# Expert tiles: second bias read from the kept table by a register, eight buffers for weight copies, and a fixed order of the steps on two engines

## The chip, the cores and the metric

The kernel runs on one core of a Trainium2 chip. The metric is device time in microseconds, the median of three runs. A core has a matrix engine (TensorE, PE in the profile), an element-wise engine (VectorE, DVE), an engine for activation functions (ScalarE, ACT), a general engine that here issues the indirect transfers and masks (GpSimd, POOL), and SyncE (SP), whose queue here issues all other DMAs. Each engine takes its own queue in order; engines wait for each other by semaphores.

## The reference

The input x is 8 x 512 x 128 in float32. Three blocks follow each other, each with a residual: half a feed-forward layer, attention with 16 heads of 8, and half a feed-forward layer again. The feed-forward layer routes each row to 2 of 8 experts:

```python
xn = (x - mu) * jax.lax.rsqrt(var + EPS) * ln_gamma + ln_beta
abel_out = _gelu(xn @ abel_w + abel_b)
logits = xn @ moe_gate_w + moe_gate_b
topw, topi = jax.lax.top_k(logits, K)
topw = jax.nn.softmax(topw, axis=-1)
...
h = _gelu(jnp.einsum('bsd,edh->ebsh', xn, ew1) + eb1[:, None, None, :])
eo = jnp.einsum('ebsh,ehd->ebsd', h, ew2) + eb2[:, None, None, :]
moe_out = jnp.einsum('ebsd,bse->bsd', eo, w_dense)
for i in range(NROT):
    moe_out = moe_out @ expm(gens[i])
...
mixed = abel_out * (1.0 - gate) + moe_out * gate
```

An expert has weights of 128 x 256 and 256 x 128 and two biases. The three rotations are the same for all rows, so the kernel multiplies them into the second weights and the second bias once.

## The kernel before

**A table of experts.** `rec` (line 130) is kept in SBUF: for each of 8 experts, 645 floats in each of 128 partitions. They are the first weights, the first bias, the second weights times the rotations (from `E_W2`) and the second bias times the rotations (129 floats from `E_B2` to `RECORD`, the same in every partition). The 129th column serves the gate.

**Sorting.** The 8 batches are two groups of 4. For each group `f_sort` (line 364) computes where each of a row's two copies goes, so that rows of one expert lie together in slots of 256 rows. There are 23 slots (`TILES`), and `whose` tells the expert of each slot. `f_send` (line 461) scatters rows to `xd` in DRAM by GpSimd.

**Expert tiles.** `f_experts(n, g, ...)` (line 504) runs the 23 tiles of layer n and group g, so there are four stretches of 23 tiles, 92 in all. A step s of its loop does four things: `fetch(s + 4)` (line 508) loads the expert's number from `whose` into a register of SyncE (L509), copies the record that it names from `rec` into a buffer `r` (L511) and loads the 256 rows `xr` from DRAM (L513); `turn(s)` transposes the rows on TensorE (`px`) and scales them on VectorE (`xs`, L532); `first(s - 1, ...)` multiplies by the first weights (`ph`) and takes the gelu on ScalarE (L546); `second(s - 3)` (line 550) multiplies by the second weights (`po`), adds the bias on VectorE (`y`, L561) and stores to `yd` in DRAM (L564). Records have 5 buffers (`AHEAD + 1`), `xr` 5, `y` 3.

**Gathers and mixes.** When a group's tiles are done, `f_fetch` (line 588) gathers each row's two results from `yd` by GpSimd, 8 gathers a batch (L599), and `f_mix` (line 604) weighs and adds them on VectorE (L613 to L624). In the first layer a batch's buffers `ye` have one copy, in the second two. In the program's text the first group's four mixes stand between the two stretches of tiles of a layer, and in the second layer each mix is followed by the store of the output (L628), by SyncE. In the first layer the second group's mixes are tasks within attention (line 884), which writes the maxima of each unit through SyncE (`qs<-mr`, L940).

**What sets the order.** A scheduler orders each engine's instructions by its own costs. `pin` (line 181, `tc.keep_in_program_order`) keeps instructions in the order of the text among those pinned on the same engine. Pinned before are all matrix products and transposes, GpSimd's gathers, scatters and masks, and one activation; VectorE's and SyncE's work around the expert tiles is not.

Of the kernel before, what the change touches and what calls it, by code (L numbers as in the profile page):

```python
# [8 lines left out]
F32 = mybir.dt.float32  # L9
I32 = mybir.dt.int32  # L10
AF = mybir.ActivationFunctionType
ALU = mybir.AluOpType
# [4 lines left out]
P = 128  # L17
# [4 lines left out]
NE = 8  # L22
# [9 lines left out]
SLOTS, CHUNKS = 256, 2  # L32
TILES = (2 * GROUP * S + NE * (SLOTS - 1)) // SLOTS
AHEAD = 4
# [4 lines left out]
PO = P + 1  # L39
E_B1, E_W2 = NHH * P, NHH * P + NHH  # L40
E_B2 = E_W2 + NHH * PO
RECORD = E_B2 + PO
# [14 lines left out]
def tile_macaron(  # L57
# [19 lines left out]
    nc = tc.nc  # L77
    V, A, G, T = nc.vector, nc.scalar, nc.gpsimd, nc.tensor
# [51 lines left out]
    rec = const.tile([P, NE, RECORD], F32, name="rec", tag="rec")  # L130
# [15 lines left out]
    for i in range(2):  # L146
# [5 lines left out]
        out=mask_q[:, S - P :], in_=mask_q[:, S - P :], pattern=[[-1, P]],  # L152
# [10 lines left out]
        out=less, in_=less, pattern=[[1, P]], compare_op=ALU.is_gt, fill=-1.0,  # L163
# [11 lines left out]
        out=before_e, in_=before_e, pattern=[[1, NE], [-1, NE]], compare_op=ALU.is_gt, fill=0.0,  # L175
# [5 lines left out]
    pin = tc.keep_in_program_order  # L181

    def mm(*args, **kw):
        pin(T.matmul(*args, **kw))  # L184

    def tp(*args):
        pin(T.transpose(*args))  # L187
# [315 lines left out]

    def f_experts(n, g, pools, tasks):
        whose = sorts[n, g][1]
        got, key = {}, f"back{n}_{g}"

        def fetch(t):
            e = nc.sync.value_load(whose[0:1, t : t + 1], min_val=0, max_val=NE - 1)  # L509
            r = pools["sb"].tile([P, RECORD], F32, name=f"r{n}_{g}_{t}", tag="record", bufs=AHEAD + 1)  # L510
            nc.sync.dma_start(out=r, in_=rec[:, bass.ds(e, 1), :].rearrange("p o c -> p (o c)"))  # L511
            xr = pools["sb"].tile([P, CHUNKS, P], F32, name=f"xr{n}_{g}_{t}", tag="xr", bufs=AHEAD + 1)
            d = nc.sync.dma_start(  # L513
                out=xr,
                in_=xd[g][t * SLOTS : (t + 1) * SLOTS, :].rearrange("(c p) d -> p c d", p=P),
            )

            for name in sent[n, g]:
                tc.add_manual_dep(
                    d.ins, name,  # L520
                    mybir.DependencyInfo(mybir.DependencyClass.Sync, mybir.DependencyReason.DATA),
                    reason="sorted rows",
                )
            got[t] = [r, xr]

        def turn(t):
            r, xr = got[t]
            pt = pools["misc"].tile([P, CHUNKS, P], F32, name=f"px{n}_{g}_{t}", tag="misc")
            for c in range(CHUNKS):
                tp(pt[:, c, :], xr[:, c, :], ident)  # L530
            xT = pools["sb"].tile([P, SLOTS], F32, name=f"xs{n}_{g}_{t}", tag="xsT", bufs=3)
            V.tensor_scalar(  # L532
                xT, pt.rearrange("p c q -> p (c q)"),
                cs[:, C_GAMMA : C_GAMMA + 1], cs[:, C_BETA : C_BETA + 1], ALU.mult, ALU.add,
            )
            got[t].append(xT)

        def first(t, c):
            r, xT = got[t][0], got[t][2]
            if c == 0:  # L540
                got[t].append(
                    pools["sb"].tile([P, NHH, SLOTS], F32, name=f"hs{n}_{g}_{t}", tag="hs", bufs=3)
                )
            ph = pools["hid"].tile([P, S], F32, name=f"ph{n}_{g}_{t}_{c}", tag="hid")
            mm(ph[:, :SLOTS], r[:, c * P : (c + 1) * P], xT, start=True, stop=True)
            A.activation(  # L546
                got[t][3][:, c, :], ph[:, :SLOTS], AF.Gelu, bias=r[:, E_B1 + c : E_B1 + c + 1]
            )

        def second(t):  # L550
            r, hs = got[t][0], got[t][3]
            po = pools["out"].tile([P, CHUNKS, PO], F32, name=f"po{n}_{g}_{t}", tag="out")
            for c in range(CHUNKS):
                for k in range(NHH):
                    mm(
                        po[:, c, :], hs[:, k, c * P : (c + 1) * P],
                        r[:, E_W2 + k * PO : E_W2 + (k + 1) * PO],
                        start=(k == 0), stop=(k == NHH - 1),
                    )
            y = pools["sb"].tile([P, CHUNKS, PO], F32, name=f"y{n}_{g}_{t}", tag="y", bufs=3)  # L560
            V.tensor_tensor(  # L561
                y, po, r[:, E_B2:RECORD].unsqueeze(1).to_broadcast([P, CHUNKS, PO]), ALU.add
            )
            nc.sync.dma_start(  # L564
                out=yd[g][t * SLOTS : (t + 1) * SLOTS, :].rearrange("(c p) d -> p c d", p=P),
                in_=y,
            )
            del got[t]

        for t in range(AHEAD):  # L570
            fetch(t)
        for s in range(TILES + 3):
            if s + AHEAD < TILES:
                fetch(s + AHEAD)
            if s < TILES:
                turn(s)
            if 0 <= s - 1 < TILES:
                first(s - 1, 0)
                first(s - 1, 1)
            if 0 <= s - 3 < TILES:  # L580
                second(s - 3)
            for f, *args in tasks.pop(s, ()):
                f(*args)
        assert not tasks

    back = {}
# [43 lines left out]
    def f_first(between):  # L630
# [52 lines left out]
        with ExitStack() as ph:  # L683
            pools = f_pools(0, ph)
            f_experts(0, 0, pools, {})
            for b in groups[0]:
                for t in range(TT):
                    f_fetch(0, b, t, work, 1)
                f_mix(0, b, False)
            f_experts(0, 1, pools, between(pools["misc"]))  # L690
# [9 lines left out]
    def f_second():  # L700

        with ExitStack() as ph:
            pools = f_pools(1, ph)
            n, b = 1, NB - 1
            sides = {b: f_beside(n, b, pools["hid"], pools["misc"], pools["sb"]) for b in range(NB)}

            def side(b):
                next(sides[b], None)

            tasks = {  # L710
                0: [(f_norm, n, b)],
                1: [(f_turn, n, b, pools["misc"])],
                2: [(f_logits, n, b, pools["misc"])],
                3: [(f_sort, n, 1, pools["misc"])],
                4: [(f_send, n, i, t) for i in range(GROUP, NB) for t in range(TT)],
                5: [(f_half, n, b)],
            }
            for i in range(NB):
                tasks.setdefault(5 + 2 * i, []).append((side, i))
                tasks.setdefault(6 + 2 * i, []).append((side, i))  # L720
            f_stats(n, (b,))
            f_experts(n, 0, pools, tasks)
            for b in range(GROUP):
                for t in range(TT):
                    f_fetch(n, b, t, pools["sb"], 2)
                f_mix(n, b, True)
            f_experts(n, 1, pools, {})
            for b in range(GROUP, NB):
                for t in range(TT):
                    f_fetch(n, b, t, pools["sb"], 2)  # L730
                f_mix(n, b, True)
# [449 lines left out]
```

## Time and profile before

| | |
|---|---|
| median of 3 runs | 1014.27 us (1010.85 to 1017.79) |
| profiled execution | 1012.17 us |
| its span | 1010.1 us |
| TensorE busy | 800.7 us (79%) |
| VectorE busy | 546.6 us (54%) |
| ScalarE busy | 446.9 us (44%) |
| GpSimd busy | 348.7 us (35%) |
| first expert stretch | 124.7 to 189.2 us |
| second, with the first group's mixes | 189 to 288 us |
| attention | 288 to 796 us |
| third expert stretch | 796 to 880 us |
| fourth, with the first group's mixes | 880 to 958 us |
| last gathers and mixes | 958 to 1010 us |

The profile is of one execution. A line of a timeline gives the start in us, the duration in us, the engine, the source line, the operation, and what it writes and reads; in brackets stands the idle time of the engine before it and what ended it. A "q" after an engine's name marks its sequencer: waits, register work and DMA issues. A line of waits gives the waiter, whom it waited for, the total in us, how often, and the longest. The stretches in the table are cut at the first record copy and the end of the last `y` of each.

### The profile page before, as it was taken

Reading aid. Unit: us, or ns where it says so; the run is one execution under the profiler, and the core shown is the slowest. Engines: PE = TensorE matmul, PEld = TensorE weight load, DVE = VectorE, ACT = ScalarE, POOL = GpSimd, SP = SyncE. Lnnn points to the kernel's source line nnn. Section 1 sums busy time; section 2 is a strip of 40 time slices with the busy share of each in tenths; the row PEclk is TensorE's granted clock in tenths of the full one; section 3 lists DMA queues with packets and bytes.
Section 4 is the critical chain, followed back from the end, with each engine's and each line's share of the span. In section 5 each row is a group of like instructions: output and inputs, shape, how many; then the busy total and the mean of one; then the engine's idle time right before and its main releaser. Section 6 shows DMA issues by size and latency. Waiting matters only on the chain.

```text
span 1010.1 us, 17346 instructions
## 1 busy us (share of the span) xinstructions
PE 800.7 (79%) x5546; PEld 554.1 (55%) x5546; DVE 546.6 (54%) x2049; ACT 446.9 (44%) x928; POOL 348.7 (35%) x421
## 2 busy tenths in 40 slices
PE   4569888767668689999999967999999779956800
PEld 4469777656545345555555533455655578845800
DVE  5855533254338565676767672676773253445323
ACT  2434233235203355767676732666766434412300
POOL 4277700245034521121212138332111047074075
PEclk9579989978766777999999975999999789978955
DMA  9973166756621300101010101201000346766622
GB/s 259 299 188 75 56 224 221 217 158 178 159 71 25 69 14 11 36 4 43 4 44 3 44 17 49 56 10 42 4 3 2 107 148 217 248 178 179 218 58 68
DMA packets 104010, 101.22 MB, mean 100 GB/s; under 512 B 11424, under 2 KB 80936, under 8 KB 103640
## 3 DMA queue, kind: packets, MB, share of 16 engines
q1 hardware_dynamic: 95728, 83.26, 28.5%
q0 software_dynamic: 8192, 16.86, 6.0%
q8 instruction: 44, 0.72, 0.3%
q14 instruction: 46, 0.38, 0.1%
HBM read 34.37 MB, written 32.89 MB: 67 GB/s over the span
## 4 chain that ended last, share of the span: by engine, by line
PE 65%; DMA 8%; issue 7%; POOL 7%; DVE 7%; SPq 3%; ACT 2%; POOLq 0%; DVEq 0%; ACTq 0%
PE sa L184 18%; PE sb L184 9%; PE py L184 8%; POOL ye L599 6%; PE ph L184 6%; PE po L184 6%; DMA ye<-yd,to 4%; DMA xr<-xd 3%; PE rp L184 3%; PE pl L184 2%; PE pyt L187 2%; PE px L187 2%; PE pp L184 2%; SPq L509 1%; PE ab L184 1%
## 5 line engine op out<-in xcount | busy, mean ns | idle before, releaser
L925 DVE CUSTOM_DVE_ANT_0 junk<-sa,mask_q 128x128 f32<-128x128 f32 (+3 forms) x512 | 251.1, 490 | 146.1 <-PE sb L184 96.4
L184 PE MATMUL sa<-ks,qs 32*128 32x128 f32 (+3 forms) x1024 | 289.9, 514 | 15.4 <-DVE mx L925 15.2
L184 PE MATMUL sb<-qs,ks 32*128 32x256 f32 (+3 forms) x1024 | 284.8, 502 | 5.5 <-DMA qs<-mr 5.5
L964 ACT ACTIVATE pr<-sb 128x384 f32<-128x384 f32 (+1 forms) x384 | 188.6, 524 | 153.9 <-PE sb L184 142.7
L599 POOL DMA_INDIRECT ye<-yd,to x128 | 123.1, 961 | 239.5 <-DMA r<-rec 68.9
L184 PEld LDWEIGHTS sa<-ks,qs 32*128 32x128 f32 x1024 | 126.6, 203 | 117.8 <-DVE mx L925 88.4
L969 POOL TENSOR_SCALAR_AFFINE_SELECT pr<-pr 128x512 f32<-128x512 f32 x128 | 80.0, 637 | 302.5 <-ACT pr L964 302.4
L468 POOL DMA_INDIRECT xd<-xh,to x128 | 125.3, 979 | 110.3 <-issue 34.6
L546 ACT ACTIVATE hs<-ph,r 128x256 f32<-128x256 f32 x184 | 82.7, 474 | 151.9 <-PE ph L184 143.4
L184 PEld LDWEIGHTS sb<-qs,ks 32*128 32x128 f32 x1024 | 136.1, 199 | 18.3 <-issue 8.1
L184 PE MATMUL ph<-xs,r 128*128 128x256 f32 x368 | 113.5, 438 | 38.2 <-issue 24.4
L184 PEld LDWEIGHTS po<-r,hs 128*128 128x128 f32 x736 | 105.2, 208 | 6.0
L184 PE MATMUL po<-r,hs 128*128 128x129 f32 x736 | 104.5, 290 | 0.0
L184 PEld LDWEIGHTS ph<-xs,r 128*128 128x128 f32 x368 | 74.1, 224 | 48.4 <-issue 40.1
L184 PE MATMUL py<-pr,va 128*32 128x512 f32 (+3 forms) x1024 | 94.8, 469 | 2.8 <-POOL pr L969 2.8
L561 DVE TENSOR_TENSOR y<-po,r 128x258 f32<-128x258 f32 x92 | 39.0, 424 | 80.3 <-PE po L184 65.9
L532 DVE TENSOR_SCALAR xs<-px,cs 128x256 f32<-128x256 f32 x92 | 49.6, 541 | 53.9 <-PE px L187 51.5
L613 DVE TENSOR_TENSOR ye<-ye,wts 128x516 f32<-128x516 f32 x32 | 22.0, 696 | 91.2 <-DMA ye<-yd,to 91.2
L187 PE MATMUL px<-ident,xr 128*128 128x128 f32 x184 | 40.7, 308 | 38.0 <-DMA xr<-xd 32.3
L620 ACT ACTIVATE gt<-gt,half_gcb 128x4 f32<-128x4 f32 x16 | 4.7, 296 | 114.9 <-DVE gt L619 114.9
L184 PEld LDWEIGHTS py<-pr,va 128*32 128x32 f32 x1024 | 24.4, 112 | 53.9 <-issue 23.0
L187 PEld LDWEIGHTS px<-ident,xr 128*128 128x128 f32 x184 | 24.1, 156 | 50.2 <-issue 31.8
(185 smaller groups left out, 850.2 us busy)
## 6 DMA issues: line engine op xcount, KB each, us to landing
r<-rec SPq DMA_DIRECT2D x92, 322.5 KB
yd<-y SPq DMA_DIRECT2D x92, 129.0 KB
xr<-xd SPq DMA_DIRECT2D x92, 128.0 KB
xd<-blank SPq DMA_DIRECT2D x2, 2944.0 KB
qkd<-qk SPq DMA_DIRECT2D x16, 256.0 KB
x<-in_x_dram SPq DMA_DIRECT2D x8, 256.0 KB
qs<-in_alibi_q_dram SPq DMA_DIRECT2D x2, 1024.0 KB
ks<-in_alibi_k_dram SPq DMA_DIRECT2D x2, 1024.0 KB
```

Of the source, the lines that this page charges most:

```text
L184: pin(T.matmul(*args, **kw))
L187: pin(T.transpose(*args))
L468: d = G.indirect_dma_start(out=xd[g], out_offset=bass.IndirectOffsetOnAxis(to[:, k, j : j + 1], 0), in_=xhs_f[n, b][:, t, :], in_offset=None,)
L509: e = nc.sync.value_load(whose[0:1, t : t + 1], min_val=0, max_val=NE - 1)
L532: V.tensor_scalar(xT, pt.rearrange("p c q -> p (c q)"), cs[:, C_GAMMA : C_GAMMA + 1], cs[:, C_BETA : C_BETA + 1], ALU.mult, ALU.add,)
L546: A.activation(got[t][3][:, c, :], ph[:, :SLOTS], AF.Gelu, bias=r[:, E_B1 + c : E_B1 + c + 1])
L561: V.tensor_tensor(y, po, r[:, E_B2:RECORD].unsqueeze(1).to_broadcast([P, CHUNKS, PO]), ALU.add)
L599: pin(G.indirect_dma_start(out=back[b][k][:, t, :], out_offset=None, in_=yd[g], in_offset=bass.IndirectOffsetOnAxis(to[:, k, j : j + 1], 0),))
L613: V.tensor_tensor(ys[k], ys[k], wts[:, k, js].unsqueeze(2).to_broadcast([P, TT, PO]), ALU.mult)
L925: V.tensor_tensor_reduce(junk[:, :n], sa[:, at : at + n], mask_q[:, S - n :], 1.0, -3.0e38, ALU.add, ALU.max, mxs[u][:, j, i : i + 1],)
L964: A.activation(pr[:, j, :], sb[:, :width], AF.Exp)
L969: pin(G.affine_select(out=pr[:, :, at : at + P], in_=pr[:, :, at : at + P], pattern=[[0, GH], [1, P]], compare_op=ALU.is_ge, fill=0.0, bas ...
```

## The change

The second bias is no longer part of a tile's copy of the record: the copy ends at `E_B2` (516 floats a partition in place of 645). For the addition of the bias VectorE loads the expert's number from `whose` into a register of its own, and reads 129 floats of `rec` at that place. The record buffers become 8 (`AHEAD + 4`). Both register loads leave out the check of bounds at run time. The loads, the record copy, the load of the rows, `xs`, `y` and the store to `yd` are pinned, so that SyncE and VectorE keep them in the order of the program's text. The mixes and the stores of the output are not pinned. `key`, which is no longer read, goes.

```diff
     def f_experts(n, g, pools, tasks):
         whose = sorts[n, g][1]
-        got, key = {}, f"back{n}_{g}"
+        got = {}
+
+        def expert(t, engine):
+
+            loads, (e,) = nc.values_load_multi_w_load_instructions(
+                whose[0:1, t : t + 1], engines=[engine], min_val=0, max_val=NE - 1,
+                skip_runtime_bounds_check_because="a count of experts, at most NE - 1 by a minimum",
+            )
+            for i in loads:
+                pin(i)
+            return rec[:, bass.ds(e, 1), :].rearrange("p o c -> p (o c)")
 
         def fetch(t):
-            e = nc.sync.value_load(whose[0:1, t : t + 1], min_val=0, max_val=NE - 1)
-            r = pools["sb"].tile([P, RECORD], F32, name=f"r{n}_{g}_{t}", tag="record", bufs=AHEAD + 1)
-            nc.sync.dma_start(out=r, in_=rec[:, bass.ds(e, 1), :].rearrange("p o c -> p (o c)"))
+            r = pools["sb"].tile([P, E_B2], F32, name=f"r{n}_{g}_{t}", tag="record", bufs=AHEAD + 4)
+            pin(nc.sync.dma_start(out=r, in_=expert(t, mybir.EngineType.SP)[:, 0:E_B2]))
...
                 in_=xd[g][t * SLOTS : (t + 1) * SLOTS, :].rearrange("(c p) d -> p c d", p=P),
             )
+            pin(d)
...
-            V.tensor_scalar(
+            pin(V.tensor_scalar(
                 xT, pt.rearrange("p c q -> p (c q)"),
                 cs[:, C_GAMMA : C_GAMMA + 1], cs[:, C_BETA : C_BETA + 1], ALU.mult, ALU.add,
-            )
+            ))
...
-            V.tensor_tensor(
-                y, po, r[:, E_B2:RECORD].unsqueeze(1).to_broadcast([P, CHUNKS, PO]), ALU.add
-            )
-            nc.sync.dma_start(
+            b2 = expert(t, mybir.EngineType.DVE)[:, E_B2:RECORD]
+            pin(V.tensor_tensor(y, po, b2.unsqueeze(1).to_broadcast([P, CHUNKS, PO]), ALU.add))
+            pin(nc.sync.dma_start(
                 out=yd[g][t * SLOTS : (t + 1) * SLOTS, :].rearrange("(c p) d -> p c d", p=P),
                 in_=y,
-            )
+            ))
             del got[t]
```

## The prediction

> **What bounds the kernel now.** I read the page's slices first, then the timeline of each of the four stretches of expert tiles, then the waits and the chain on SyncE's queue. The slices tell that TensorE is nearly full where attention runs and holed around it.
>
> ```profile
> span 1010.1 us, 17346 instructions
> PE   4569888767668689999999967999999779956800
> ```
>
> A slice is 25.25 us. Attention's are nines; the holes that this change touches are slices 7 to 11 (177 to 303 us) and 35 to 37 (884 to 960 us). There the second 23 tiles of an expert layer run beside the gathers and mixes of the first. The timeline of 200 to 210 us shows what holds the tiles:
>
> ```profile
> 202.35 0.94 POOL L599 DMA_INDIRECT ye<-yd,to  x1 [0.31 <-issue]
> ...
> 203.74 0.69 DVE L613 TENSOR_TENSOR ye<-ye,wts 128x516 f32<-128x516 f32 x1 [6.46 <-DMA ye<-yd,to]
> 204.93 0.69 DVE L613 TENSOR_TENSOR ye<-ye,wts 128x516 f32<-128x516 f32 x1 [0.49 <-DMA ye<-yd,to]
> 205.54 0.42 DVE L561 TENSOR_TENSOR y<-po,r 128x258 f32<-128x258 f32 x1
> ...
> 206.48 0.54 DVE L532 TENSOR_SCALAR xs<-px,cs 128x256 f32<-128x256 f32 x1
> ...
> 207.12 2.05 PE L184 MATMUL ph<-xs,r 128*128 128x256 f32 x4 [5.18 <-issue]
> ```
>
> VectorE takes its queue in order. A mix (L613) waits 6.46 us for a gather, the tile's `y` and `xs` stand behind it, and TensorE idles 5.18 us and comes back at half clock (2.05 us; 1.03 elsewhere). Four tiles or so slip through between two mixes: **before, gathers and tiles share the time.**
>
> Where no mix interferes, two paces compete. TensorE's, from its timeline in the last stretch, is 1.98 us a tile:
>
> ```profile
> 932.80 0.38 PE L187 MATMUL px<-ident,xr 128*128 128x128 f32 x2
> ...
> 934.78 0.38 PE L187 MATMUL px<-ident,xr 128*128 128x128 f32 x2
> ```
>
> SyncE's shows on the chain of waits where the first tiles start:
>
> ```profile
> 127.09 0.54 SPq L511
> ...
> 127.67 0.59 SPq L513
> ...
> 128.31 0.63 SPq L509
> ```
>
> Record copy 0.54, rows of x 0.59, register load 0.63: issue alone takes 2.2 us a tile here. Last, SyncE's own waits:
>
> ```profile
> SPq L511 <- DVE y L561: 63.8, 35, 7.1
> ...
> SPq L509 <- DVE whose L451: 15.1, 1, 15.1
> ```
>
> The first is the record copy waiting for a free buffer, the second the load of the second layer's table in the middle of attention.
>
> **The change, part by part.** The sum is made on the profiled execution, 1012.2 us with a span of 1010.1; the median of the runs, 1014.3, is 0.2% above it.
>
> *Eight record buffers, shorter copies.* The 63.8 us of waits go, since a record is fetched 4 steps ahead and released 3 steps after its own. What is late next is SyncE itself. A copy shrinks from 322.5 to 258 KB; the DMA share of the stretches is only 0.60 to 0.67, so I count nothing for it.
>
> *Order on SyncE.* In the changed program's built order each step is load, address, record copy, rows, `yd`. Before, a load mostly came right after a record copy and took 0.27. The bounds operations (0.15 and 0.02, with gaps 0.05 each) go. The new step, by rows of the trace: load 0.62, address 0.05, copy 0.49, rows 0.59, `yd` 0.45, two event waits of 0.03, and 0.04 after each of the seven: 2.54. I take **2.55 us**. Here two rules of the Trainium skill speak against the rows, one each way. "DMA: Bandwidth & Descriptors", section "Issuing engines are not separate DMA queues", says that the sequencer's time to start a DMA is usually small beside the DMA; by it SyncE costs nothing and tiles run at 1.98. Its section "Latency and other measured facts" gives a register load a floor of about 600 ns; the trace has 0.27 for most, so that no floor holds, but 0.58 to 0.63 after two other issues. With 0.27 the step is 2.2. In the changed order the load always follows copy, rows and `yd`, so I stay with 0.62. A fetch without `yd` (the first eight of a stretch) is 1.97.
>
> *Second bias by a register on VectorE.* 92 loads and 92 address operations. The trace has none on VectorE; the nearest row is SyncE's load, 0.26 to 0.90. An added instruction can't gain. VectorE works some 1.0 us in a 1.98 us step, and `y` waits for `po` anyway, so the four products of `po` hide it; only the last three tiles of a stretch, 0.9 us apart, let it show. I take 0; uncovered it is 1 us a stretch.
>
> *Order on VectorE and across stretches.* This is the large term. In the built order all four mixes of the first group stand ahead of the second group's first `xs`; and in the second layer SyncE issues the four output stores, each waiting for its mix, ahead of the second group's first fetch. Queued behind: every tile of the group, TensorE and ScalarE with it.
>
> *First stretch.* First copy issued at 124.66 as before; 8 x 1.97 + 15 x 2.55 = 54.0; the last rows land 1.9 after that issue ends; the last tile's path (0.4 + 0.86 + 0.9 + 0.87 + 2.69 + 0.45) 6.2; handovers 0.4: last `y` ends at 187.2. Before 189.15: **-2**.
>
> *Second stretch.* Gathers start 4.0 later (3.7 to 4.4 in the three other places), 191.2. Per batch the eighth gather starts after 8.75, lands after 2.8, multiply, add and subtract take 1.95, restart 0.4: 13.9 (14.4 to 15.7 before, with tiles between). Four: 3 x 13.9 + 8.75 + 2.8 + 3.3 for the mix's end = 56.5, so the first `xs` is at 247.7. At half clock the first `y` comes 8.3 later, 256.0. SyncE then needs 15 x 2.55 = 38.3, plus 6 for the ten issues of attention's first queries and keys and their landing, then 3.2 landing (up to 5.0 was seen there) and 6.2: 309.7. Before 288.0: **+21.7**, the first stretch included.
>
> *Attention.* The loads that sat in it go. The chain:
>
> ```profile
> 605.62 0.26 SPq L509
> ...
> 606.24 0.64 SPq L940
> ...
> 609.40 1.19 PE sb L184
> ```
>
> The maxima were ready at 599.6 and were sent only at 606.24: up to 6.6 us. But GpSimd's queue is full of scatters from 596.9 on and reaches the next mask only here:
>
> ```profile
> 618.76 0.64 POOL L969 TENSOR_SCALAR_AFFINE_SELECT pr<-pr 128x512 f32<-128x512 f32 x1
> ```
>
> TensorE waits for GpSimd at 626.3, and GpSimd's order is unchanged. I take **0**; if that cover is thinner than it looks, -6.6.
>
> *Third stretch.* TensorE and its side products set 3.26 us a step, more than 2.55. The start loses the loads taken in advance (1.97 a fetch, 1.29 before): **+1**.
>
> *Fourth stretch.* The 32 gathers run 883.8 to 923.6 as before. The last mix ends 45.7 after 883.8 (39.8 + 2.6 + 3.3); store, load and address 0.9; first copy at +46.6; then 62.6 as from 124.66 to 187.2: +109.2. Before 957.75, +73.9: **+35.3**. The closing gathers and mixes, 52.4, stay.
>
> Sum 21.7 + 0 + 1 + 35.3 = 58: **1070 us**.
>
> **The rivals.**
>
> *TensorE's pace.* The hold stays, but SyncE keeps up. First stretch: tile 6 at 141.0, 16 x 1.98 and 6.2: 178.8. Second: 239.3 + 23 x 1.98 + 4.1 of attention's products + 2 half clock + 6.2 = 297, +9. Fourth: 54.1 for 62.6: +26.8. With the third's 1, 1049. For it: the median load of 0.27, and fetches that run ahead while the mixes hold. Against: the rows above.
>
> *Slower still.* A SyncE step of 2.8 (a load of 0.9 was seen once) costs 15 x 0.25 in each of three stretches, VectorE's loads 1 us each: 1084.
>
> *Faster.* The mechanism is that the deeper prefetch carries the second group past the mixes. At SyncE's pace the second stretch would end near 246 and the fourth near 939: -42 and -19, 953. What decides is how many mixes stand ahead of the group: each costs about 14 us in the second stretch and 10 in the fourth, some 29 with the fill; none gives -60, four give +58, and two break even. The built order has four on VectorE, so this needs an order that the chip cannot choose.
>
> **How the numbers follow.** My forecast 0.57, TensorE's pace 0.22, slower still 0.18, faster 0.03. The range takes 1049 less 3 at the low end and 1084 at the high. A measurement of this kernel tells about 1% from no change. Faster by over 1% 0.02, within 1% 0.01, slower 0.97.
>
> **What the changed profile would show.** Right: VectorE's eight long waits for `ye<-yd`, with no `xs` between the mixes; TensorE idle some 55 us from about 192 and some 48 from about 885; `px` 2.5 us apart elsewhere; SyncE's wait for `y` at the record copy gone; no load around 600 us, with TensorE still late on GpSimd after 610. Wrong: `px` 2.0 us apart (then 1049), tiles running between two mixes (then the hold is misread), or attention shorter by more than 3 us.

## The result, and the profile after

The change makes the kernel slower: **1061.63 us**, median of 4 runs (1057.19 to 1065.32), against 1012.56 of the kernel before (4 runs, 1006.23 to 1017.79). The ratio is 1.0486, with an interval of 1.0405 to 1.0566. The profiled execution after took 1065.32 us, with a span of 1063.5; that of before took 1012.17. So the profiles differ by 53.2 us, where the medians differ by 49.1: two of the four runs after took some 7 us less than the other two, of which one is the profiled one.

The page of the kernel after: its span and TensorE's slices of 26.6 us.

```profile
span 1063.5 us, 17340 instructions
PE   4579889106977689999999768999997799009900
```

Where the page of before had fives to eights around 200 and 900 us there are now two holes, a 1 and 0 (slices 7 and 8, counted from 0, 186 to 239 us) and a 0 and 0 (slices 34 and 35, 904 to 957); the last two zeros are the closing gathers, as before. The first six of seven stages of that span, from the kernel after, and then the second and the fourth stretch of the kernel before; the columns after the window and its length are the busy times of PE, PEld (TensorE's weight loads), DVE, ACT and POOL, each with its number of instructions, then the granted TensorE clock (its share of full speed), the DMA share and GB/s:

```profile
0.00:132.13 132.13, 96.58 (x582) 87.54 (x582) 78.44 (x313) 44.18 (x84) 73.51 (x93) 0.77 0.58 167
132.13:188.64 56.51, 49.51 (x322) 44.84 (x322) 20.66 (x46) 20.90 (x46) 0.00 (x0) 0.94 0.67 211
188.64:310.49 121.85, 55.98 (x347) 49.95 (x350) 43.45 (x127) 34.15 (x68) 31.73 (x33) 0.72 0.46 126
310.49:819.69 509.20, 463.85 (x3524) 256.21 (x3518) 317.50 (x1326) 290.73 (x602) 149.89 (x199) 0.89 0.10 25
819.69:904.31 84.62, 72.69 (x452) 63.79 (x452) 37.66 (x113) 35.76 (x75) 30.96 (x32) 0.90 0.52 166
904.31:1011.13 106.82, 49.98 (x322) 45.09 (x322) 36.86 (x87) 22.09 (x50) 30.77 (x32) 0.73 0.48 144
```

```profile
189.15:288.02 98.87, 66.16 (x345) 57.78 (x348) 40.74 (x127) 32.33 (x67) 31.70 (x33) 0.81 0.60 164
...
879.80:957.75 77.95, 54.49 (x318) 49.20 (x318) 35.05 (x87) 21.93 (x50) 31.31 (x32) 0.87 0.67 199
```

Beside the prediction, in us (a stage's length; the stretches end with their last `y`):

| stage | before | after | change | predicted |
|---|---|---|---|---|
| opening, to the first record copy | 124.7 | 132.1 | +7.5 | 0 |
| first stretch | 64.5 | 56.5 | -8.0 | -2 |
| second stretch | 98.9 | 121.9 | +23.0 | +23.7 |
| attention | 507.6 | 509.2 | +1.6 | 0 |
| third stretch | 84.1 | 84.6 | +0.5 | +1 |
| fourth stretch | 78.0 | 106.8 | +28.9 | +35.3 |
| closing gathers and mixes | 52.3 | 52.3 | 0 | 0 |
| sum | 1010.1 | 1063.5 | +53.4 | +58 |

The two holds are where they were expected. The timeline of the kernel after at the end of the first:

```profile
244.38 2.04 DVE L622 TENSOR_TENSOR ye<-ye,wts 128x516 f32<-128x516 f32 x2 [8.14 <-DMA ye<-yd,to]
...
248.07 1.14 DVE L633 SCALAR_TENSOR_TENSOR x<-xT,gt,x 128x128 f32<-128x128 f32 x4
249.12 0.99 DVE L542 TENSOR_SCALAR xs<-px,cs 128x256 f32<-128x256 f32 x2
...
249.71 2.08 PE L184 MATMUL ph<-xs,r 128*128 128x256 f32 x4 [53.72 <-DVE xs L542]
```

The fourth mix ends, the group's first two `xs` follow at once, and TensorE starts after 53.72 us of idle time, at half clock (granted 0.50 from 249 to 253 us). The waits of TensorE from 904 to 960 us show the other hold, and whom it waits for is not the same:

```profile
PE px L187 <- DMA xr<-xd: 54.6, 2, 53.5
```

Here no rows have been fetched: SyncE stands at the output stores. In SyncE's own waits of the kernel after there is none for `y` at the record copy (63.8 us before), and the one of the output stores for the mixes has grown from 50.9 us to:

```profile
SPq L637 <- DVE x L633: 93.9, 8, 18.0
```

Between the holds tiles run faster than forecast. The chain of the kernel after in the fourth stretch, where SyncE sets it (start, us, what):

```profile
968.50 0.23 SPq L522
...
968.82 0.46 SPq L573
...
969.32 0.28 SPq L510
...
969.80 0.49 SPq L520
...
970.34 4.16 DMA xr<-xd
```

The register load (L510) behind the store (L573) takes 0.28, where 0.62 was counted. Record copies are issued 2.19 us apart (median in the first and in the fourth stretch), not 2.55. TensorE runs off at its own 1.98 us a tile, overtakes SyncE, and then stands for one landing of rows, as here: its transposes `px` start 1.99 us apart in the first stretch and 2.05 in the fourth by the median, 2.12 and 2.16 by the mean.

### The profile page after: what moved, and what is told of

Read it like the earlier page. It is cut to its first block, busy times and chain, and to the rows that moved or that the text cites. A ratio compares the mean times of both kernels' runs of the same rounds, so it can differ in the third digit from the quotient of the medians.

```text
span 1063.5 us, 17340 instructions
## 1 busy us (share of the span) xinstructions
PE 788.6 (74%) x5546; PEld 547.4 (51%) x5546; DVE 550.9 (52%) x2049; ACT 449.0 (42%) x929; POOL 347.6 (33%) x421
## 4 chain that ended last, share of the span: by engine, by line
PE 65%; POOL 10%; DMA 9%; issue 6%; DVE 6%; SPq 1%; ACT 1%; POOLq 0%; DVEq 0%; ACTq 0%
PE sa L184 16%; PE sb L184 8%; POOL ye L608 8%; PE py L184 8%; PE ph L184 7%; PE po L184 7%; DMA ye<-yd,to 4%; PE rp L184 3%; DMA xr<-xd 3%; PE px L187 2%; PE pl L184 2%; POOL xd L468 2%; PE pyt L187 2%; PE pp L184 1%; PE ab L184 1%
## 5 line engine op out<-in xcount | busy, mean ns | idle before, releaser
L184 PE MATMUL ph<-xs,r 128*128 128x256 f32 x368 | 104.7, 411 | 53.7 <-DVE xs L542 53.7
L187 PE MATMUL px<-ident,xr 128*128 128x128 f32 x184 | 40.6, 306 | 83.1 <-DMA xr<-xd 80.7
L184 PEld LDWEIGHTS po<-r,hs 128*128 128x128 f32 x736 | 98.0, 196 | 4.6
L184 PEld LDWEIGHTS ph<-xs,r 128*128 128x128 f32 x368 | 68.9, 209 | 60.5 <-DVE xs L542 54.1
L572 DVE TENSOR_TENSOR y<-po,rec 128x258 f32<-128x258 f32 x92 | 39.3, 427 | 114.9 <-PE po L184 74.5
L184 PE MATMUL po<-r,hs 128*128 128x129 f32 x736 | 98.4, 279 | 0.0
## 6 DMA issues: line engine op xcount, KB each, us to landing
qkd<-qk SPq DMA_DIRECT2D x16, 256.0 KB
x<-in_x_dram SPq DMA_DIRECT2D x8, 256.0 KB
```

The source lines that it names most:

```text
L572: pin(V.tensor_tensor(y, po, b2.unsqueeze(1).to_broadcast([P, CHUNKS, PO]), ALU.add))
```

## The experiments

Eleven kernels were run, each beside runs of the kernel before. Four questions: what holds the tiles, what sets SyncE's step, what the other parts of the change are worth, and whether the order can be had without the hold. The first is seen best in the order that VectorE's queue was built with. A dot is a tile's `xs`, an M a mix (where a mix is in pieces, its first):

```
                          second stretch                 fourth stretch
before                    ....M....M....M....M.......    ......M.M..M..M............
after                     MMMM.......................    MMMM.......................
no order (e1)             .....M....M....M....M......    ......M.M..M..M............
order on SyncE only (e2)  ..M.....M....M....M........    MMMM.......................
mixes placed (e3)         .......M.......M....M.....M    ........M.....M.....M.....M
in pieces (e7)            ......M.......M.......M...M    .......M.....M.....M.....M.
```

**No order at all (e1).** All of the change but the pins.

```diff
-            pin(V.tensor_scalar(
+            (V.tensor_scalar(
...
-            for i in loads:
-                pin(i)
```

(So for `xs`, `y`, the loads, the copy, the rows and the store.)

> The change with nothing pinned on VectorE and SyncE; the short copies, the eight buffers and the register on VectorE stay. In the built order the four mixes stand after 5, 9, 13 and 17 of the second group's tiles in the first layer, and after 6, 7, 9 and 11 in the second, nearly as before the change. Theory (the whole loss is the order, the rest of the change costs nothing): about the time of the kernel before, 1005 to 1020 us, second stretch some 99 us from the last y before it to its own last y, fourth some 78. Rival (the register load on VectorE or the shorter, more frequent copies cost): some 10 us more a stretch of tiles, 1030 us or more. Rival (eight buffers free the tiles): faster than before by over 1%, under 1000 us.

Measured: 996.37 us, ratio to before 0.985 (0.971 to 0.999). The two stretches in the kernel without the order:

```profile
187.13:268.56 81.43, 58.69 (x345) 52.09 (x348) 40.71 (x126) 31.82 (x67) 31.71 (x33) 0.87 0.64 179
...
853.82:932.35 78.53, 54.06 (x318) 49.07 (x318) 35.27 (x86) 21.91 (x50) 31.13 (x32) 0.85 0.60 170
```

The whole loss is gone with the order, as the theory has it, and more: the second stretch is 17.4 us shorter than before the change, so that the total comes out as the last rival said. The four runs spread, 986 and 990 us at a mean granted clock of 0.87, 1003 and 1009 at 0.86 and 0.84. What is left of the change is no cost but a gain, of 1.5% over all four runs and some 2.3% in the first two.

**Order on SyncE only (e2).** `xs`, `y` and VectorE's loads are not pinned.

```diff
             for i in loads:
-                pin(i)
+                if engine == mybir.EngineType.SP:
+                    pin(i)
```

> The change with the order kept on SyncE alone; xs, y and the register loads of VectorE are not pinned. In the built order the first layer's mixes stand after 2, 7, 11 and 15 of the second group's tiles, the second layer's four still ahead of its tiles, with the four output stores ahead of the second group's first fetch on SyncE. Theory (two holds with two causes: in the second stretch it is VectorE's order, in the fourth SyncE's stores alone would do it): second stretch back near before's 99 us, fourth still about 107, so 1035 to 1045 us. Rival (VectorE's order makes both): both back, 1010 to 1020. Rival (SyncE's order makes both): both stay, 1060.

Measured: 1027.61 us, ratio 1.016 (1.007 to 1.024). The two stretches:

```profile
185.48:278.70 93.22, 63.98 (x347) 56.12 (x350) 40.94 (x126) 32.09 (x67) 31.70 (x33) 0.82 0.63 165
...
865.51:973.21 107.70, 49.70 (x322) 44.91 (x322) 37.84 (x87) 22.09 (x50) 30.68 (x32) 0.75 0.47 143
```

Second stretch 93.2, fourth 107.7: as the theory said for both, while the total is 7 us below its range, much of it in the first stretch, 58.0 us here and 64.5 before. So the change has **two holds with two causes**. In the first layer VectorE's order makes it. In the second SyncE's order is enough: four output stores, each behind its mix, stand ahead of the next group's fetches, and with no rows there is nothing that VectorE could do first. A kernel with VectorE's order alone was not run, so whether that order is enough for a hold, in either layer, stays open.

**Copies with five buffers (e5).** The kernel of e1 with the old number of buffers.

```diff
-tag="record", bufs=AHEAD + 4)
+tag="record", bufs=AHEAD + 1)
```

> The kernel of the run without order (nothing pinned on VectorE and SyncE), with five buffers for the copies of records in place of eight; short copies and the register on VectorE stay. The mixes stand after 4, 9, 13 and 17 of the second group's tiles in the first layer. Theory (of the second stretch's gain of 17.4 us against the kernel before, 98.9 to 81.4, all is the eight buffers'): SyncE waits for y at the record copy again, second stretch 95 to 99 us, total 1005 to 1020. Rival (the gain is of the shorter copy or of the order that the scheduler now takes): second stretch stays at 81 to 85, total as with eight buffers, 990 to 1000.

Measured: 1006.15 us, ratio 0.990 (0.983 to 0.997), in the range of the first theory. But it doesn't settle the shares. By the ratios 1% of e1's 1.5% is there with five buffers too, and so belongs to the shorter copy or the scheduler's new order. But four of e5's five runs lie at 1003 to 1006 us, and the two shortest of e1 at 986 and 990; by these most of the gain is the buffers'. By the second stretch, 94.3 us here and 81.4 in e1, nearly three quarters of that stretch's gain is the buffers'; but this profile is of the longest of e5's runs (1022.69 us), with a clock of 0.78 in that stretch where e1 had 0.87. Both parts gain something; how much each, stays open.

**Rows ahead of the register load (e4).** To see what SyncE's load costs behind what.

```diff
         def fetch(t):
-            r = pools["sb"].tile([P, E_B2], ..., bufs=AHEAD + 4)
-            pin(nc.sync.dma_start(out=r, in_=expert(t, ...)[:, 0:E_B2]))
             xr = ...
             pin(d)
...
+            r = pools["sb"].tile([P, E_B2], ..., bufs=AHEAD + 4)
+            pin(nc.sync.dma_start(out=r, in_=expert(t, ...)[:, 0:E_B2]))
             got[t] = [r, xr]
```

> The change with one thing moved: each fetch issues the load of the rows ahead of the register load and the record copy, so that SyncE's order is store, rows, register load, copy in place of store, register load, copy, rows. Theory (a register load takes 0.55 to 0.6 us right behind the issue of the rows and 0.27 behind a store to yd or a copy): median load 0.56, the tiles of the last stretch 2.45 us apart for 2.18, that stretch 4 us longer. Rival (the load takes 0.27 whenever SyncE is in its steady pace, whatever stands ahead): median load 0.27, tiles 2.18 apart, no change.

Measured: 1073.21 us in one run; fourth stretch 111.5 us for 106.8, first 61.6 for 56.5, copies 2.50 us apart. The register loads of this kernel, and below those of the change (minimum, median, maximum in ns):

```profile
L510 SPq TENSOR_LOAD <-whose x92: 263/557/867, 131.9 to 1009.5; - x92
```

```profile
L510 SPq TENSOR_LOAD <-whose x92: 262/278/780, 87.8 to 1001.3; - x92
L510 DVEq TENSOR_LOAD <-whose x92: 296/310/609, 141.9 to 1009.8; - x92
```

The theory holds, with the step at its size: with the same short copies the load takes twice as long right behind the rows as behind a store. In its step, 2.50 for 2.55, this kernel is the one that the prediction described.

**The full record with the order (e6), and with the register too (e9).** e6 reads the bias from the tile's copy again, with no load on VectorE; e9 has the long copy and the load.

```diff
-            r = pools["sb"].tile([P, E_B2], ..., bufs=AHEAD + 4)
+            r = pools["sb"].tile([P, RECORD], ..., bufs=AHEAD + 4)
-            pin(nc.sync.dma_start(out=r, in_=expert(t, ...)[:, 0:E_B2]))
+            pin(nc.sync.dma_start(out=r, in_=expert(t, ...)))
...
-            b2 = expert(t, mybir.EngineType.DVE)[:, E_B2:RECORD]
+            b2 = r[:, E_B2:RECORD]
```

(The last two lines in e6 alone.)

> The change with the second bias read from the tile's own copy again: the copy is 645 floats a partition, VectorE has no register load; eight buffers and the order on both engines stay. Theory (the register load on VectorE lies beside its own work, and the shorter copy saves nothing that is waited for): the time of the change, 1055 to 1066 us, tiles 2.18 us apart, the same holds. Rival (a load and an address operation cost VectorE 0.4 us a tile that shows, up to 1 us a stretch in the drain and more where VectorE is busy): 4 to 15 us less than the change.

Measured: 1077.57 us, ratio 1.059 (1.048 to 1.070): 16 us **more** than the change by the medians, 11 by the ratios, which neither theory had. Copies stood 2.46 us apart, and the load behind a store took 0.52 us. That gave the next expectation.

> The change with the record copies of 645 floats a partition; VectorE's register load, eight buffers and the order stay, so that against the run with the full record only the register load is put back. Theory (it is the longer copy that makes SyncE's register load behind a store take 0.52 us in place of 0.27, and so its step 2.46 in place of 2.19): 1070 to 1085 us, load behind a store 0.5, copies 2.46 us apart. Rival (the register load on VectorE in place of the copied bias was what saved time, or those runs had a lower clock): 1055 to 1066, load 0.27, copies 2.19 apart.

Measured: 1077.86 us, ratio 1.064 (1.055 to 1.074). The loads of e9:

```profile
L510 SPq TENSOR_LOAD <-whose x92: 264/532/858, 85.2 to 1005.8; - x92
L510 DVEq TENSOR_LOAD <-whose x92: 299/322/886, 136.9 to 1015.1; - x92
```

With and without VectorE's register load the medians are within 0.3 us (far inside the intervals), and no stretch of tiles is longer in e9 than in e6, so that load costs nothing that shows. The copy's length is worth some 12 to 16 us of the pinned kernel, 12 by the four stretches of e9's profile and 16 by the medians: with 645 floats SyncE's load behind a store takes 0.51 us and the step 2.45, with 516 floats 0.27 and 2.19. Why a longer copy, with the rows and the store issued after it, lengthens a register load isn't shown by any run.

**Mixes placed between the tiles (e3).** All of the change stays; the first group's gathers and mixes become tasks of the second group's steps, pinned, and each output store stands two steps behind its mix.

```diff
+MIX_0 = (6, 13, 20, 25)
+MIX_1 = (7, 12, 17, 22)
...
-            for b in groups[0]:
-                for t in range(TT):
-                    f_fetch(0, b, t, work, 1)
-                f_mix(0, b, False)
-            f_experts(0, 1, pools, between(pools["misc"]))
+            tasks = between(pools["misc"])
+            gather(0, 0, work, 1)
+            for b in groups[0]:
+                tasks.setdefault(MIX_0[b], []).append((f_mix, 0, b, False))
+                if b + 1 < GROUP:
+                    tasks[MIX_0[b]].append((gather, 0, b + 1, work, 1))
+            f_experts(0, 1, pools, tasks)
```

> The change with one thing moved in the text: the first group's mixes (pinned on VectorE) and their gathers are put between the second group's tiles, after 7, 14, 18 and 23 tiles in the first layer and after 8, 13, 18 and 23 in the second; each output store stands two steps behind its mix. Theory (the hold is the loss, and the pinned steps themselves run at some 2.2 us a tile): the second stretch takes 23 x 2.2 and 7 of fill and drain, 58 us for 122, the fourth 59 for 107; a mix takes some 4 us of VectorE of which half shows, 8 us a stretch: 960 to 975 us. Rival (gathers and tiles share the DMA queues or GpSimd so that tiles starve anyway): no better than before, 1005 to 1020. Rival (the pinned order of SyncE is itself the cost): over 1040.

Measured: 982.32 us, ratio 0.972 (0.964 to 0.980). So the pinned order isn't the cost; where the mixes stand in it is. But the two stretches take 79.3 and 76.2 us, not the 66 and 67 that the theory gives with its 8 us of mixes. The timeline of e3 shows what a mix does:

```profile
870.89 1.29 DVE L631 TENSOR_TENSOR ye<-ye,wts 128x516 f32<-128x516 f32 x2
...
874.27 1.14 DVE L642 SCALAR_TENSOR_TENSOR x<-xT,gt,x 128x128 f32<-128x128 f32 x4
875.33 0.54 DVE L544 TENSOR_SCALAR xs<-px,cs 128x256 f32<-128x256 f32 x1
...
875.97 1.33 PE L186 MATMUL ph<-xs,r 128*128 128x256 f32 x4 [2.92 <-issue]
```

It waits for no gather; it just keeps VectorE for 4.4 us, an `xs` stands behind it, and TensorE stops and comes back slower. I had let half of it hide; the fourth stretch exceeds the 59 us without mixes by 17, as much as four whole mixes.

**Mixes in pieces (e7).** `f_mix` becomes four pieces behind the `y` of four steps.

```diff
+            yield
         pin(V.tensor_add(m, m, ys[1]))
...
+                mix = mix_pieces(n, b)
+                for k in range(4):
+                    tasks.setdefault(MIX_1[b] + k, []).append((next, mix))
```

> The kernel with the mixes between the tiles, each mix cut into four pieces that stand behind the y of four successive steps (two products; sum and gate; gate and difference; four updates of x), the first piece after 6, 13, 20 and 23 tiles in the first layer and after 7, 12, 17 and 22 in the second. Theory (in one piece a mix keeps VectorE 4.4 us, xs stands behind it, and four of them are the 17.6 us by which the fourth stretch, 76.2 us, exceeds 23 steps of 2.18 and the fill and drain; in pieces of at most 1.3 us they fit into what VectorE has free of a step): fourth stretch 60 to 64 us, second 64 to 70, total 945 to 960. Rival (gathers that land 8 us after their issue among the tiles' own transfers, or the transfers themselves, set that stretch): no gain over the mixes in one piece, 975 to 985.

Measured: 982.44 us, ratio 0.968 (0.958 to 0.977). The fourth stretch is 65.7 us for e3's 76.2, a little above the theory's 60 to 64. The second, with 83.1, missed it, and so did the total. The timeline of e7 shows why:

```profile
268.15 0.69 DVE L631 TENSOR_TENSOR ye<-ye,wts 128x516 f32<-128x516 f32 x1 [6.44 <-DMA ye<-yd,to]
269.45 0.70 DVE L631 TENSOR_TENSOR ye<-ye,wts 128x516 f32<-128x516 f32 x1 [0.60 <-DMA ye<-yd,to]
270.06 0.42 DVE L574 TENSOR_TENSOR y<-po,rec 128x258 f32<-128x258 f32 x1
```

The fourth batch's two products stand ahead of the last three `y` and wait for their gathers: the change's own fault, in small.

**The old copies with the right order (e8).** e7 with the record of 645 floats, five buffers and no register.

```diff
-            r = pools["sb"].tile([P, E_B2], ..., bufs=AHEAD + 4)
+            r = pools["sb"].tile([P, RECORD], ..., bufs=AHEAD + 1)
```

> The kernel with the mixes in pieces, with the record copies as before the change: 645 floats, five buffers, no register on VectorE; only the order is left of the change. Theory (a record lives from 4 steps ahead of its tile to 3 behind; with five buffers its copy can only go out two steps ahead, and two steps of 2.2 us are just what issue and landing take): SyncE waits for y at the record copy, tiles 2.4 to 2.8 us apart, 8 to 15 us more in each of the three stretches that run at SyncE's pace, 970 to 1000. Rival (with a right order five buffers do as well, the buffers add nothing): within 5 us of the mixes in pieces with eight buffers.

Measured: 1122.74 us, ratio 1.102 (1.092 to 1.112), far beyond both. Copies stand 4.5 us apart in the first stretch. SyncE's waits of e8 for `y` at the record copy, which the change had taken away, and its timeline there:

```profile
SPq L522 <- DVE y L574: 164.6, 65, 7.9
```

```profile
168.60 0.43 DVE L574 TENSOR_TENSOR y<-po,r 128x258 f32<-128x258 f32 x1 [3.69 <-DMA yd<-y]
169.09 0.49 SPq L522 DMA_DIRECT2D r<-rec  x1
169.63 0.58 SPq L524 DMA_DIRECT2D xr<-xd  x1
170.27 0.50 SPq L575 DMA_DIRECT2D yd<-y  x1
...
173.06 0.43 DVE L574 TENSOR_TENSOR y<-po,r 128x258 f32<-128x258 f32 x1 [3.59 <-DMA yd<-y]
```

It is a circle of one tile. The copy waits for a record buffer, which `y` frees; rows and then the store to `yd` are issued behind the copy; the next `y` waits until that store has landed and given one of the three `y` buffers back. The scheduler's order before the change issued the store of tile t - 7 ahead of the copy for tile t, not behind it, and had no such circle. Three things differ from e7; the copy's length was worth 12 to 16 us in e9 and VectorE's load nothing, so most of the 140 us is left to the buffers. With five buffers and no order (e5) the kernel took 1006 us, so a fixed order and the eight buffers belong together: neither can be judged alone.

**Last obstacles (e10), and the stores by another engine (e11).** e10 is e7 with the fourth mix of the first layer behind its stretch, and attention's first transfers behind SyncE's last fetch; e11 adds one word.

```diff
-            15: [(spread, 0, 0, psum)],
-            16: [(spread, 0, 1, psum)],
+            20: [(spread, 0, 0, psum)],
+            21: [(spread, 0, 1, psum)],
...
+            f_mix(0, GROUP - 1, False)
```

```diff
-            pin(nc.sync.dma_start(
+            pin(nc.scalar.dma_start(
                 out=yd[g]...
```

> The kernel with the mixes in pieces, and two things moved in the first layer's second stretch: the fourth batch's mix stands behind the last tile, and the products, transfers and values for attention's first batch are put from steps 15, 16 and 18 to 20, 21 and 22, behind SyncE's last fetch (the first batches' first pieces stand at steps 5, 13 and 21). Theory (that stretch, 83.1 us for 65.7 in the fourth, loses 8 us to SyncE waiting for attention's transfers among its fetches and 11 to the two last y standing behind a product that waits for the fourth batch's gathers): second stretch 64 to 69 us, of which up to 5 come back at the start of attention; total 955 to 968. Rival (the gathers' pace sets it, or attention starts later by as much): no gain, 975 to 985.

> The kernel of the run before in this list with one thing moved: the stores to yd are issued by ScalarE in place of SyncE. Theory (without the stores SyncE's step is 1.97 us, below TensorE's 1.98, though its register load then stands behind the rows and takes 0.56): tiles of the first stretch 2.0 us apart for 2.15, first stretch 3 us shorter, the others 1 to 3; total 948 to 965. Rival (a store waits on ScalarE's queue for y, and the gelus behind it wait too): slower by 5 to 20 us.

Measured: e10 973.59 us, ratio 0.954 (0.946 to 0.963), second stretch 73.2 us, fourth 66.4; the direction is the theory's, the size is some 4 us short in the stretch and 6 in the total. The two moves were not run apart. The profile is of the longest of e10's runs (983.13 us), with attention at a clock of 0.86; in the two stretches its clock is that of e11 (0.90 and 0.95 for 0.90 and 0.94). e11: **957.65 us, ratio 0.940 (0.933 to 0.948)**, the fastest kernel of all. The stages of e11 from the first to the fourth stretch:

```profile
124.38:181.84 57.46, 49.47 (x326) 45.16 (x326) 20.80 (x47) 19.74 (x46) 0.05 (x1) 0.94 0.80 242
181.84:244.73 62.89, 54.46 (x334) 48.80 (x334) 35.16 (x101) 30.98 (x66) 25.14 (x27) 0.90 0.73 202
...
842.86:901.18 58.32, 48.84 (x318) 44.74 (x318) 34.69 (x86) 21.39 (x50) 30.96 (x32) 0.94 0.78 223
```

The copies of the first stretch are 1.97 us apart, as worked out, with a load of 0.59 behind the rows; the first stretch gains 1.8 us for the 3 expected. The two with mixes gain far more, 10.3 and 8.0. What they gain is TensorE's waiting for rows, which goes from 9.0 us to nothing in the second stretch. In the fourth, from e10 and then from e11:

```profile
PE px L189 <- DMA xr<-xd: 13.0, 11, 4.4
```

```profile
PE px L189 <- DMA xr<-xd: 0.3, 1, 0.3
```

So the rows come in time once the stores are off SyncE. How much of that is the shorter step, and how much that SyncE no longer stands at a store for a late `y` with the next fetch behind it, isn't shown.

## Why the prediction was right, and where it wasn't

The forecast of 1070 us has its sign and its main mechanism right: 53.4 us in the profile for 58, and 1061.63 lies in the range. Some of this is luck: 7.5 of the 53.4 us are the opening's, which the sum had at 0 and the change doesn't touch. From the first record copy on the change cost 45.9 us for the 58. Step by step:

- **The order across the stretches: right.** First `xs` of the second group at 249.1 (predicted 247.7), first `y` at 256.5 (256.0). In the fourth stretch the first copy came 46.3 us after the gathers' start (46.6). e1 takes both holds away with the order, and e2 the first of them with VectorE's part of it alone.
- **The order on SyncE, 2.55 us a step: the step that failed.** The term is the register load, "I stay with 0.62". It measured 0.27, because in the changed order a store lies between it and the rows, and because the copy is short; the step is 2.19. Behind the rows (e4) the load takes 0.56, and with the long copy behind a store (e9) 0.51. In the fourth stretch this is 15 x 0.36 = 5.4 us; the last `y` came 103.7 us after the gathers' start for the 109.2 predicted. In the trace of before the tiles' loads of 0.6 us mostly have the rows directly ahead of them, or a store and directly ahead of that the record copy. Copy, rows and store, as in the changed order, stood ahead of a load there twice (with another load between), at 231.05 and 255.25 us, and it took 0.35 and 0.27: a duration was carried over without its neighbours.
- **"I count nothing" for the shorter copy: wrong in this kernel.** e9 shows that it is worth 12 to 16 us once SyncE's step bounds the tiles. It comes as SyncE's time: with the long copy the load takes 0.24 us more and the step 0.26.
- **The two rules of the Trainium skill.** "DMA: Bandwidth & Descriptors", section "Issuing engines are not separate DMA queues", calls the sequencer's time to start a DMA usually small relative to the DMA itself. That is so here (in the chain above 0.49 us for an issue, and 4.16 until the rows land); that SyncE then costs nothing, as the forecast read it, doesn't follow. Issues are 1.5 us of a step of 2.19, and copies stood 2.19 us apart. The floor of 600 ns for a register load (section "Latency and other measured facts") doesn't hold: the median of 92 is 278 ns, the smallest 262.
- **Second bias on VectorE at 0: right.** e6 against e9 has the load without and with, 1077.57 and 1077.86. The load need not even wait for the products of `po`: in the kernel after 88 of the 92 loads lie almost wholly beside an operation of VectorE's own, and by the median a load ends 1.4 us ahead of its `y`.
- **First stretch, -2: right in sum only.** The stretch lost 8.0 us, for the same 0.36 us a step, and the opening grew by 7.5, which has nothing to do with the change (below).
- **Second stretch, +23.7: right in sum (+23.0), by two errors.** The shorter step should have taken 5.4 off it. Against that the hold was 1.1 longer than counted, and the last rows, fetched beside attention's first transfers, came late: from the end of the last rows' issue (297.1) to the last `y` (310.5) it took 13.4 us for the 9.4 counted.
- **Attention, 0: right, with its cover.** The stall of the maxima at 606 us is gone: none waits for the second layer's table any more. GpSimd's scatters now hide it, as told. The timeline of the kernel after:

```profile
638.68 0.96 POOL L468 DMA_INDIRECT xd<-xh,to  x1 [0.30 <-issue]
639.65 0.64 POOL L978 TENSOR_SCALAR_AFFINE_SELECT pr<-pr 128x512 f32<-128x512 f32 x1
...
640.35 1.51 PE L184 MATMUL py<-pr,va 128*32 128x384 f32 x8 [11.36 <-POOL pr L978]
```

  TensorE arrives earlier at the same mask and waits 11.36 us for it; before, its waits for masks from 590 to 640 us came to 2.8. A stall was taken away, and the time stayed with the engine behind it.
- **The rivals.** TensorE's pace (1049 us) came nearer than the forecast in the stretches where nothing holds: 56.5 us in the first, for its 54.1 and the forecast's 62.5, and 103.7 after the gathers' start in the fourth, for its 100.7 and 109.2. Of the forecast's own signs `px` 2.5 us apart did not come; 1.99 and 2.05 is the sign that it had named for this rival. Less the 7.5 us of the opening, the profile's 1012.2 and 45.9 make 1058, between 1049 and 1070. A step of 2.8 was seen nowhere in the change. The faster case named its own condition, no mix ahead of the second group; e3, e7, e10 and e11 meet it. That e11 comes to 957.65 where 953 was worked out is no confirmation of that sum, for e11 also cuts the mixes and takes the stores off SyncE.

## What to carry to other kernels

An order written out by hand is an order of everything on that queue: before pinning some steps, list what else stands on it and waits (here mixes behind gathers, and stores behind mixes), and place those too, in pieces no longer than the engine's free time in a step. Take a duration from the trace together with its neighbours on the queue, for a moved instruction has new ones. A fixed order and the number of buffers must be judged together, for a wait that a scheduler would have stepped around closes a circle in a fixed one.

## What the runs showed of the hardware

**A register load's time depends on what was issued before it, and how long before.** On SyncE it took 0.27 us behind a store to `yd` and 0.56 behind the load of the rows (kernel after, e4), and 0.51 behind the store when the record copy ahead of rows and store was 645 floats a partition for 516 (e9). In e9 the 36 such loads whose copy had been issued 1.2 us before took 0.38 to 0.63 us, and 20 of the 22 with 1.5 us or more between took 0.26 to 0.35. What the load waits for isn't shown. On VectorE a load took 0.31 us (kernel after), beside the arithmetic.

**The clock moves whole stages from run to run.** Up to the first record copy the orders of all five engines are the same in both kernels; the window of 55 to 65 us had a granted clock of 0.97 in the profile of before, and in that of after:

```profile
55.00:65.00 10.00, 8.27 (x37) 7.79 (x37) 2.10 (x7) 1.55 (x2) 7.56 (x9) 0.50 0.74 169
65.00:75.00 10.00, 7.44 (x34) 6.74 (x32) 4.30 (x14) 0.78 (x1) 7.66 (x8) 0.50 0.71 230
```

Just before it the last scaled rows of the second group's routing start at nearly the same time in both (54.9 and 55.1 us); just behind it the first copy of `z` stands at 79.5 and 87.0. So the 7.5 us came about at half clock; why the clock was lower in one execution isn't shown. All profiles split by it: with 0.50 in that first window the first copy is at 132 to 134 us (after, e4, e6, e7, e8), with 0.86 to 1.00 at 124 to 128 (the others). The four runs after lie at 1057 and 1058 and at 1065 and 1065, which fits the two openings, though only one of them has a profile. Attention, with the same products, took 503.7 us at a granted clock of 0.91 (e4), 507.6 at 0.89 (before) and 521.5 at 0.87 (e5). A single run therefore can't show an effect of some 10 us; a stage can, beside its clock.
